# A graph layer with a mixture of experts on one core: the last chunk's slot tiles placed earlier, and the additions of results counted by gathers issued

## Chip, cores and metric

One core of one Trainium2 chip runs the whole kernel. The metric is device time in microseconds (us) of one execution. Six runs of the kernel before gave a median of 1196.74 us, from 1194.26 to 1201.27. One more execution was profiled: it took 1194.66 us, of which the profile covers a span of 1192.9 us.

The engines are named as in the profile: PE (TensorE), DVE (VectorE), ACT (ScalarE), POOL (GpSimd) and SP (SyncE). SP issues most of the plain transfers and POOL all the gathers.

## The reference

`x` has 6250 rows of 256 numbers, and there are 100000 edges `src -> dst`, sorted by `dst`.

```python
x = x + gnn(layernorm(x), edges, W, b)       # [h, mean of h[src] over the edges into a node] @ W.T + b
h = layernorm(x)
xn = layernorm(h) * gamma + beta
logits = xn @ Wr + br                        # 8 experts; the best two, softmax over those two
y = sum over the two: w_e * (gelu(xn @ W1[e] + b1[e]) @ W2[e] + b2[e])
x = x + y
```

Everything is float32. W1 is 256 x 512 for each expert, W2 is 512 x 256.

## The kernel before

**Windows, chunks, batches.** The edges are cut into 56 windows of 14 edge tiles (`C = 14`), 128 edges each. For an edge tile POOL gathers 128 rows of `z_d` (L601) into one of 28 buffers `xg` (`XG = 28`), issued 28 edge tiles ahead, and PE multiplies it with a one-hot matrix `hot` (L618). DVE makes the `hot` tiles of a window in two halves of seven (`hot_tiles`, L612). Four windows make a chunk (`CW = 4`); the 14 chunks lie in three batches of 8, 5 and 1 chunks (`BATCHES`).

**Routing a chunk.** When a window's sums stand in PSUM, DVE makes its new rows x1 (`window_x1`, L658 to L660). Behind a chunk's fourth window come: norms and logits, the choice of two experts, and the counts of tokens for each expert (`count_tokens`, L678 to L693). Then `one_hot_slots` (L697, L698) makes a tile `to` of 128 x 256 for each of the four windows on DVE, `sort_tokens` (L705, L708) multiplies the normed rows by it on PE and copies the result to `xs` on ACT. On DVE, `share_runs`, `place_rest` and `place_runs` (L727 to L780) work out where each expert's tokens go. ACT then copies the tokens to the experts' slots `xe` (`copy_runs`, L859). `find_rows` (L809 to L822) makes the plan: for each token the two rows of `y_d` with its results, and the two weights. `put_plan` (L826) writes it to DRAM in four transfers on SP; each of them overlaps the one before and so waits for its landing. `load_plans` (L841) reads it back.

**Experts.** A chunk's experts run in pairs (`expert_stages`: L884 and L889 for the hidden layer, L897 and L901 for the result, and a write of 256 rows to `y_d`, L903). Tokens beyond 128 for an expert go to rest tiles, which run behind a batch's last chunk (`more_stages`: L927 and L931, L936 and L939, L945 and L949, and a write to `y_d`, L952). The second batch has five rest tiles, the third two. The tiles `rows`, which L901, L931 and L949 write, rotate through three buffers; the PSUM tile `py` has one.

**Results.** The 49 node tiles of 128 rows are finished last. `gather_rows` loads x1 of a tile (L973, SP) and issues two gathers from `y_d` (L976, POOL): 98 in all. `add_rows` makes two additions with weights on DVE (L983) and writes the tile to the output (L985, SP). A tile's three buffers are taken in turn from the 28 of `xg`, so a buffer comes round again after nine node tiles. The gathers of a batch read `y_d` up to that batch's end, and so wait for its last write: 54 gathers are for the first batch, 36 for the second, 8 for the third.

**The order of work** is written by hand: every engine, SP's and POOL's queues among them, takes its instructions in the order in which this Python code issues them. One step of `after(t)` goes with each of the 784 edge tiles; when those are over, steps go on until nothing is left. `at(t, f)` puts a piece of work at a step; the tables `Steps`, `LateSteps` and `LastSteps` say at how many steps behind a chunk's last edge tile its pieces come. `after` also issues expert stages, paced by estimates of their times that it adds up in `clock`, and calls `sum_rows`. This issues the gathers of the next node tile when `clock` has reached `due`, and decides when the additions of earlier node tiles (the list `adds`) are issued.

In the kernel before, no addition is issued while edge tiles are left, unless more than eight node tiles wait (`XG // 3 - 1`). Behind them one is issued each time that `clock` has passed `added`, which goes up by 2.5 for each.

The last chunk, number 14, uses `LastSteps`: its four `to` tiles are issued at steps 13, 14, 17 and 18, its four sorts at 15, 16, 19 and 20, with `share_runs` at 15, `place_rest` at 16, `place_runs` at 19, the copies to slots from 21 on, `find_rows` at 22, and the first expert stages at 29.

Of the kernel before, what the change touches and what calls it, by code (L numbers as in the profile page):

```python
# [8 lines left out]
F32 = mybir.dt.float32  # L9
# [8 lines left out]
P = 128  # L18
EPS = 1e-5
C = 14  # L20
TB = 4
UB = 2
CW = 4
# [4 lines left out]
XG = 28  # L28
# [5 lines left out]
def gnn_ffn_kernel(ctx: ExitStack, tc: tile.TileContext, x, x_cols, src, dst, dst_next, gw, gw_t, gb, gb_cols, gamma, beta,  # L34
# [42 lines left out]
    W = src.shape[1]  # L77
# [511 lines left out]
    work = fast_pools.enter_context(tc.tile_pool(name="work", bufs=2, side="right"))  # L589
# [103 lines left out]
        nc.vector.tensor_scalar(q2, q2, -1.0, None, op0=ALU.add)  # L693

    def one_hot_slots(G, i):
        to = work.tile([P, 2 * P], F32, name="to", bufs=3)
        nc.vector.tensor_scalar(to, cols, G.to[:, 0, i:i + 1], None, op0=ALU.is_equal)  # L697
        nc.vector.scalar_tensor_tensor(to, cols, G.to[:, 1, i:i + 1], to, op0=ALU.is_equal, op1=ALU.add)  # L698
        G.one_hot[i] = to
# [269 lines left out]
    def gather_rows(K, n, V):  # L969
        V.rows = slice(n * P, min((n + 1) * P, N))  # L970
        count = V.rows.stop - V.rows.start
        V.o = spare()[:count]
        nc.sync.dma_start(V.o, x1_d[V.rows, :])  # L973
        V.y2 = [spare()[:count] for _ in range(2)]
        for r in range(2):
            nc.gpsimd.indirect_dma_start(  # L976
                out=V.y2[r], out_offset=None, in_=y_d[:K.batch.end_row, :],
                in_offset=bass.IndirectOffsetOnAxis(ap=plans[:count, n, r:r + 1], axis=0))

    def add_rows(n, V):  # L980
        count = V.rows.stop - V.rows.start
        for r in range(2):
            nc.vector.scalar_tensor_tensor(V.o, V.y2[r], plans.bitcast(F32)[:count, n, 2 + r:3 + r], V.o,  # L983
                                           op0=ALU.mult, op1=ALU.add)
        nc.sync.dma_start(out[V.rows, :], V.o)  # L985
# [3 lines left out]

    tasks, later, Ks, sums, adds = [], {}, [], [], []  # L990
    slots, w1_sb, w2_sb, xe = None, None, None, None
    now, spent, clock, due, added, spares = None, 0.0, 0.0, 0.0, 0.0, 0
    class Steps:

        x1, var, roots, norms, route, exps, weigh, choices, count = 2, 5, 7, 9, 11, 14, 15, 16, 19
        hot, sort = (22, 24, 26, 28), (26, 28, 30, 32)
        runs, rest, place, tiles, copied, rows, pace, start, apart = 30, 33, 36, 39, 40, 46, 1.5, 60, 2

    class LateSteps:

        x1, var, roots, norms, route, exps, weigh, choices, count = 2, 4, 5, 7, 9, 11, 12, 13, 15
        hot, sort = (17, 18, 20, 22), (19, 21, 23, 25)
        runs, rest, place, tiles, copied, rows, pace, start, apart = 20, 22, 24, 27, 26, 28, 1.25, 36, 1

    class LastSteps:

        x1, var, roots, norms, route, exps, weigh, choices, count = 2, 4, 5, 6, 7, 8, 9, 10, 12
        hot, sort = (13, 14, 17, 18), (15, 16, 19, 20)
        runs, rest, place, tiles, copied, rows, pace, start, apart = 15, 16, 19, 24, 21, 22, 1, 29, 1

    def at(t, f, *args):
        later.setdefault(max(t, now), []).append(lambda: f(*args))
# [1 line left out]
    def window_done(V, G, K, t):  # L1014
# [26 lines left out]
        for m in range(CW):  # L1041
            at(t + S.hot[m], one_hot_slots, G, m)
            at(t + S.sort[m], sort_tokens, G, m)
# [19 lines left out]

    def sum_rows():

        nonlocal due, added
        if now < W * C:
            added = clock + 3.0
        while adds and now >= W * C and (added <= clock or not (sums or tasks)):
            adds.pop(0)()  # L1070
            added += 2.5
        left = W * C - 1 - now
        while sums and not sums[0][0].batch.left and clock >= due and left < XG:
            if 0 < left < XG and spares + 3 > XG - left:
                return
            K, n = sums.pop(0)
            V = Group()
            gather_rows(K, n, V)
            adds.append(lambda n=n, V=V: add_rows(n, V))
            while len(adds) > XG // 3 - 1:  # L1080
                adds.pop(0)()
                added += 2.5
            due = max(due, clock - 6.0) + (4.0 if left > 0 else 2.4)

    def after(t):
        nonlocal now, spent, clock
        now = t
        while later.get(t):
            later[t].pop(0)()
        later.pop(t, None)  # L1090
        clock += 0.6 if t < W * C else 0.3 if tasks else 1.2

        pace = 0.6 if W * C - 56 <= t < W * C else 0.72 if t < W * C else 1.2 if len(Ks) < W // CW else 2.0
        spent = min(spent + pace, pace) if tasks else 0.0
        while tasks and spent > 0:
            us, f, _ = tasks.pop(0)
            spent -= us
            clock += us
            f()
        sum_rows()  # L1100
# [7 lines left out]
    now = 0  # L1108
# [62 lines left out]
    with tc.If(wrong_r > 0), tc.tile_pool(name="gp", bufs=1) as gp:  # L1171
# [9 lines left out]
        with tc.For_i(0, W * C) as j:  # L1181
# [22 lines left out]
            to = gp.tile([P, 1], I32, name="to")  # L1204
# [107 lines left out]
```

## Time and profile before

| what | us |
|---|---|
| six runs, median (lowest to highest) | 1196.74 (1194.26 to 1201.27) |
| the profiled execution: its own time | 1194.66 |
| its span in the profile | 1192.9 |
| busy: PE, PE's weight loads, DVE, ACT, POOL | 1055.5, 857.6, 687.9, 463.1, 843.8 |
| first and last start of the 98 gathers of results | 1049.9, 1180.5 |

The page lists for each engine its busy time, its share of 40 equal slices, the chain of work that ended last, and the costliest groups of instructions. The times of a timeline are us from the span's start. A line of it gives start, duration, engine, source line, operation, tiles and count; in brackets stand the idle time of the engine before it and what ended it. A row of windows gives for a stretch each engine's busy time, and behind them the share of full speed that the clock of PE was granted.

### The profile page before, as it was taken

What the parts mean: (1) busy time and instruction counts of PE and PEld (TensorE: products, weight loads), DVE (VectorE), ACT (ScalarE), POOL (GpSimd) and SP (SyncE); (2) the same over time, 40 slices, a digit from 0 to 9 for tenths busy, and PEclk for the clock granted to TensorE, in tenths of its full rate; (3) what the DMA queues carried; (4) which work ended last, traced back from release to release, by engine and by line L of the source; (5) the groups of instructions that cost most, each with busy time, mean ns of one, the idle gap of its engine ahead of it and who ended that gap; (6) DMA issues with size and microseconds to landing.
All of it is one profiled execution on the core that took longest, in us unless ns stands there. A gap on an engine that the chain in (4) does not pass through costs nothing.

```text
span 1192.9 us, 18881 instructions
## 1 busy us (share of the span) xinstructions
PE 1055.5 (88%) x5352; PEld 857.6 (72%) x5352; DVE 687.9 (58%) x2433; ACT 463.1 (39%) x1281; POOL 843.8 (71%) x892
## 2 busy tenths in 40 slices
PE   7939986899989989798998989899999999997970
PEld 6728765687868778686876868578888888785750
DVE  5747778564745645364564537465472745657652
ACT  3420002635434434344443444444553553643510
POOL 0077677777777777777777777777777777777674
PEclk9969988999999989899999999999999999998995
DMA  9978989546565555645555465555656564676874
GB/s 326 350 237 265 294 269 355 126 140 146 145 134 141 145 127 141 146 138 136 144 147 128 140 144 143 135 146 141 139 137 157 145 146 133 144 209 214 220 243 129
DMA packets 143578, 210.08 MB, mean 176 GB/s; under 512 B 36652, under 2 KB 111128, under 8 KB 143340
## 3 DMA queue, kind: packets, MB, share of 16 engines
q0 software_dynamic: 42768, 118.91, 40.4%
q1 hardware_dynamic: 92364, 80.45, 21.3%
q10 hardware_dynamic: 8336, 9.45, 2.4%
q8 instruction: 45, 0.74, 0.3%
q14 instruction: 65, 0.53, 0.1%
HBM read 163.86 MB, written 44.86 MB: 175 GB/s over the span
## 4 chain that ended last, share of the span: by engine, by line
PE 61%; DMA 14%; DVE 8%; ACT 4%; issue 3%; POOL 1%; ACTq 1%; SPq 0%; POOLq 0%; DVEq 0%
PE pS L618 21%; PE ph L884 16%; PE py L897 14%; DMA xg<-z_d,src_i 5%; PE pm L705 4%; DMA xg<-y_d,plans 3%; ACT xe L859 3%; DMA u_d<-u_t 3%; PE pS L621 2%; DMA plan_d<-plan 1%; PE ph L927 1%; PE py L945 1%; DMA x<-u_d 1%; DVE xe L863 1%; DVE xg L983 1%
## 5 line engine op out<-in xcount | busy, mean ns | idle before, releaser
L601 POOL DMA_INDIRECT xg<-z_d,src_i x770 | 731.7, 950 | 240.3 <-issue 103.6
L618 PE MATMUL pS<-xg,hot 128*128 128x265 f32 x1568 | 437.9, 404 | 53.9 <-DMA xg<-z_d,src_i 30.5
L618 PEld LDWEIGHTS pS<-xg,hot 128*128 128x128 f32 x1568 | 289.4, 195 | 135.1 <-DMA xg<-z_d,src_i 48.7
L884 PEld LDWEIGHTS ph<-xe,w_sb 128*128 128x128 f32 x1792 | 221.1, 196 | 13.1 <-ACT xe L859 4.5
L884 PE MATMUL ph<-xe,w_sb 128*128 128x128 f32 x1792 | 223.9, 280 | 2.9 <-ACT xe L859 2.9
L897 PE MATMUL py<-w_sb,hid 128*128 128x256 f32 x896 | 214.4, 383 | 1.8 <-DVE rows L901 1.8
L612 DVE TENSOR_TENSOR hot<-cols,rel 128x896 f32<-128x896 f32 x112 | 121.6, 1087 | 129.9 <-PE pS L618 127.3
L889 ACT ACTIVATE hid<-ph,b_sb 128x128 f32<-128x128 f32 x448 | 127.5, 368 | 173.3 <-PE ph L884 173.0
L897 PEld LDWEIGHTS py<-w_sb,hid 128*128 128x128 f32 x896 | 169.0, 191 | 33.3 <-issue 6.8
L859 ACT ACTIVATE xe<-xs x448 | 139.3, 311 | 86.3 <-ACT xe L859 36.6
L976 POOL DMA_INDIRECT xg<-y_d,plans x98 | 96.4, 984 | 36.1 <-issue 14.9
L708 ACT ACTIVATE xs<-pm,beta_sb,gamma_sb 128x256 f32<-128x256 f32 x112 | 57.1, 560 | 130.9 <-PE pm L705 130.5
L901 DVE TENSOR_TENSOR rows<-py,b_sb 128x512 f32<-128x512 f32 x56 | 38.4, 686 | 115.2 <-PE py L897 115.1
L640 ACT ACTIVATE sums<-pS 128x265 f32<-128x265 f32 x55 | 21.3, 388 | 114.2 <-PE pS L618 110.9
L271 PE MATMUL ph<-gc,x_t 128*128 128x264 f32 (+1 forms) x200 | 58.1, 416 | 8.1 <-ACT zt L295 5.0
L660 DVE SCALAR_TENSOR_TENSOR x<-pS,rdeg,x 128x264 f32<-128x264 f32 x55 | 27.1, 493 | 65.8 <-DMA x<-u_d 64.3
L705 PE MATMUL pm<-to,xn 128*128 128x256 f32 x224 | 58.6, 385 | 5.6 <-DVE to L698 5.6
L983 DVE SCALAR_TENSOR_TENSOR xg<-xg,plans,xg 128x256 f32<-128x256 f32 (+1 forms) x98 | 46.0, 485 | 21.9 <-DMA xg<-y_d,plans 18.1
L330 POOL DMA_INDIRECT xg<-x_dram,src_i x14 | 13.4, 958 | 61.0 <-DMA src_i<-src_dram 57.1
L271 PE MATMUL pm<-gc,x_t 128*128 128x264 f32 (+1 forms) x192 | 54.4, 408 | 0.0
L889 ACT ACT_TABLE_LOAD x25 | 32.1, 1283 | 56.3 <-PE ph L884 56.0
L271 PEld LDWEIGHTS ph<-gc,x_t 128*128 128x128 f32 x200 | 39.6, 202 | 18.8 <-ACT zt L295 5.9
(214 smaller groups left out, 892.1 us busy)
## 6 DMA issues: line engine op xcount, KB each, us to landing
y_d<-rows SPq DMA_DIRECT2D x56, 256.0 KB
xg<-z_d,src_i POOLq DMA_INDIRECT x770
w_sb<-w_dram ACTq DMA_DIRECT2D x16, 512.0 KB
x<-u_d SPq DMA_DIRECT2D x55, 132.0 KB
x_d<-x SPq DMA_DIRECT2D x55, 128.0 KB
u_d<-u_t SPq DMA_DIRECT2D x24, 264.0 KB
x_t<-x_cols_dram SPq DMA_DIRECT2D x12, 512.0 KB
xu<-x_dram SPq DMA_DIRECT2D x24, 256.0 KB
```

The costliest lines, as they stand in the source:

```text
L271: nc.tensor.matmul(pz, x_t[:, t, k, :], gc[:, h * KD + k, :n], start=(k == 0), stop=(k == KD - 1))
L601: nc.gpsimd.indirect_dma_start(out=xg[(g * C + c) % XG][:, :DZ], out_offset=None, in_=z_d[:, :], in_offset=bass.IndirectOffsetOnAxis(ap=sr ...
L612: nc.vector.tensor_tensor(hot, col[:, None, :].to_broadcast([P, HC, P]), V.rel[:, c:c + HC, None].to_broadcast([P, HC, P]), op=ALU.is_equal)
L618: nc.tensor.matmul(V.pS, V.hot[c // HC][:, c % HC, :], xg[(V.g * C + c) % XG], start=(c == 0), stop=(c == C - 1))
L705: nc.tensor.matmul(px[:, k, :], G.xn[i][:, k * P:(k + 1) * P], G.one_hot[i], start=True, stop=True)
L708: nc.scalar.activation(xs[:, at:at + 2 * P], px[:, k, :], AF.Identity, bias=beta_sb[:, k:k + 1], scale=gamma_sb[:, k:k + 1])
L859: nc.scalar.activation(xe[:, :, bass.ds(to_at, CAP)], src[:, :, bass.ds(src_at, CAP)], AF.Copy)
L884: nc.tensor.matmul(ph[:, i, a * SH:(a + 1) * SH], w1_sb[:, U.e + a, k, c * P:(c + 1) * P], xe[:, k, at:at + SH], start=(k == 0), stop=(k = ...
L889: nc.scalar.activation(U.hid[:, c, a * SH:(a + 1) * SH], ph[:, i, a * SH:(a + 1) * SH], AF.Gelu, bias=b1_sb[:, U.e + a, c:c + 1])
L897: nc.tensor.matmul(U.py[:, h, :], U.hid[:, c, h * P:(h + 1) * P], w2_sb[:, U.e + h, c, :], start=(c == 0), stop=(c == KH - 1))
L976: nc.gpsimd.indirect_dma_start(out=V.y2[r], out_offset=None, in_=y_d[:K.batch.end_row, :], in_offset=bass.IndirectOffsetOnAxis(ap=plans[:c ...
L983: nc.vector.scalar_tensor_tensor(V.o, V.y2[r], plans.bitcast(F32)[:count, n, 2 + r:3 + r], V.o, op0=ALU.mult, op1=ALU.add)
```

## The change

Three edits.

1. The tiles `to` get four buffers (`CW`) in place of three.
2. `LastSteps` places the last chunk's four `to` tiles at steps 13, 13, 14 and 15 and its sorts at 14 to 17; `share_runs`, `place_rest` and `place_runs` come at 16, 17 and 18, the copies from 20 on, `find_rows` at 21, the expert stages at 28.
3. `sum_rows` keeps no estimated time for additions. A node tile's additions are issued when more than three node tiles have had their gathers issued and wait for additions (more than five in the steps from the end of the edge tiles to the last chunk's last sort). This holds while edge tiles are left as well.

```diff
     def one_hot_slots(G, i):
-        to = work.tile([P, 2 * P], F32, name="to", bufs=3)
+        to = work.tile([P, 2 * P], F32, name="to", bufs=CW)
...
     class LastSteps:
         x1, var, roots, norms, route, exps, weigh, choices, count = 2, 4, 5, 6, 7, 8, 9, 10, 12
-        hot, sort = (13, 14, 17, 18), (15, 16, 19, 20)
-        runs, rest, place, tiles, copied, rows, pace, start, apart = 15, 16, 19, 24, 21, 22, 1, 29, 1
+        hot, sort = (13, 13, 14, 15), (14, 15, 16, 17)
+        runs, rest, place, tiles, copied, rows, pace, start, apart = 16, 17, 18, 24, 20, 21, 1, 28, 1
...
     def sum_rows():
-        nonlocal due, added
-        if now < W * C:
-            added = clock + 3.0
-        while adds and now >= W * C and (added <= clock or not (sums or tasks)):
+        nonlocal due
+        waiting = 5 if W * C <= now < W * C + LastSteps.sort[-1] else 3
+        while adds and (len(adds) > waiting or not (sums or tasks)):
             adds.pop(0)()
-            added += 2.5
         left = W * C - 1 - now
...
             adds.append(lambda n=n, V=V: add_rows(n, V))
-            while len(adds) > XG // 3 - 1:
-                adds.pop(0)()
-                added += 2.5
             due = max(due, clock - 6.0) + (4.0 if left > 0 else 2.4)
```

What this does to the order of the built program, engine by engine: up to the second batch's last stretch nothing moves. On DVE the two additions of node tile 0 come to stand ahead of the second half of the last window's `hot` tiles (they stood behind that window's expert results), and the additions of node tiles 1 to 5 ahead of that window's L658 (before: tiles 0 and 1). Tiles 6 to 10 stand between there and the counts (before: 2 to 7). The four `to` tiles come in a row, with two node tiles' additions among them; before, the third and fourth stood behind `place_rest` and an L931. On PE the four sorts (L705) come ahead of most of the second batch's L927. On SP the second write of a rest tile (L952) comes to stand behind the fourth `put_plan`; before, it stood behind the third. On POOL the 98 gathers keep their order.

More of the change, by code (lines that the diff above doesn't have):

```diff
@@ L991, in gnn_ffn_kernel @@
     slots, w1_sb, w2_sb, xe = None, None, None, None
-    now, spent, clock, due, added, spares = None, 0.0, 0.0, 0.0, 0.0, 0
+    now, spent, clock, due, spares = None, 0.0, 0.0, 0.0, 0
     class Steps:
```

## Prediction

> **What bounds the kernel now.** All that the change moves lies behind 1040 us, so I read the end first: the chain of work that ended last, in order of time.
>
> ```profile
> 1145.31 7.06 DMA xg<-y_d,plans x2
> 1153.07 16.19 DMA xg<-y_d,plans x5
> 1170.90 5.27 DMA xg<-y_d,plans
> 1180.50 5.97 DMA xg<-y_d,plans
> ```
>
> Its rows are start and time spent. The end hangs on gathers of results. POOL's timeline shows why:
>
> ```profile
> 1049.89 0.94 POOL L976 DMA_INDIRECT xg<-y_d,plans  x1 [0.30 <-PE pS L618]
> 1051.14 0.94 POOL L976 DMA_INDIRECT xg<-y_d,plans  x1 [0.30 <-DMA xg<-z_d,src_i]
> ...
> 1117.88 0.94 POOL L976 DMA_INDIRECT xg<-y_d,plans  x1 [3.87 <-DMA out_dram<-xg]
> ...
> 1124.95 0.94 POOL L976 DMA_INDIRECT xg<-y_d,plans  x1 [1.52 <-DVE xg L983]
> ```
>
> 98 gathers stand in one queue, one each 1.25 us (0.94 and 0.30), from 1049.89 on. 97 steps would take 121.3 us; the last started at 1180.50, after 130.6. Some 6.2 us of the rest are four stops above the usual 0.30 (0.69 at 1109.14, 3.57, 0.73 and 1.22), the others are single slow starts. The gather at 1124.95 is number 55, the first for the second batch: it needs that batch's last write to `y_d`. SP's timeline (start, time that the entries last, number of transfers) shows when that went out:
>
> ```profile
> 1105.01 0.35 SPq L826 DMA_DIRECT2D plan_d<-plan  x1
> ...
> 1109.13 3.39 SPq L826 DMA_DIRECT2D plan_d<-plan  x2
> 1112.61 0.38 SPq L952 DMA_DIRECT2D y_d<-rows  x1
> ...
> 1116.04 0.34 SPq L826 DMA_DIRECT2D plan_d<-plan  x1
> ...
> 1119.77 0.93 SPq L952 DMA_DIRECT2D y_d<-rows  x2
> ```
>
> The last write was issued at 1120.3. With some 3.5 us to land (1120.3 to 1123.8) it explains 1124.95, though the profile names DVE. So the stops at 1109 to 1121 are hidden: without them POOL would stand at gather 55 until the same moment. **The second batch's last write to y_d, then POOL's queue, sets the end.** The first of the last chunk's gathers, number 91, started at 1170.90; that chunk's last L952 was issued at 1159.5. There are some 9 us of slack.
>
> **Part 1: additions by gathers issued (edit 3).** DVE takes its queue in order, so an addition issued early holds all behind it until its gather has landed.
>
> ```profile
> 1046.17 1.09 DVE L612 TENSOR_TENSOR hot<-cols,rel 128x896 f32<-128x896 f32 x1 [6.31 <-PE pS L618]
> ...
> 1061.73 0.15 DVE L658 TENSOR_SCALAR rdeg<-pS 128x1 f32<-128x1 f32 x1
> ```
>
> *First wait.* Node tile 0's two additions now stand ahead of this `hot` tile. Its second gather starts at 1051.14; a gather on the chain took 3.64 us (`1088.07 3.64 DMA xg<-y_d,plans` among its rows): 1054.8. One addition (0.48) and the tile (1.09): ready at 1056.4, not 1047.3. PE needs it for the last window's eighth edge tile, at 1052.7 (three edge tiles in 1.51 us from 1052.22). **PE stands for 3.7 us**, with the expert matmuls queued behind. After such an idle stretch PE runs slowly for a while; the windows of 1074 to 1082 show it behind an idle time of 3.64 us (a row has the busy time of PE, its weight loads, DVE, ACT and POOL, then PE's granted clock, the DMA engines' busy share and GB/s):
>
> ```profile
> 1074.00:1078.00 4.00, 1.89 (x8) 1.66 (x9) 3.76 (x15) 1.46 (x5) 3.08 (x4) 0.86 0.96 325
> 1078.00:1082.00 4.00, 3.12 (x10) 2.06 (x10) 2.35 (x7) 0.00 (x0) 3.09 (x4) 0.72 0.50 149
> ```
>
> The granted clock falls to 0.86 and 0.72, and eight L897 matmuls took 3.52 us there against 1.89 later: +1.6 to +2.2. So the last window's sums come 5.3 to 5.9 later.
>
> *Second wait.* Tiles 1 to 5 are added ahead of L658. Tile 5's second gather is number 12: 1049.89 + 11 x 1.25 = 1063.6, landed 1067.3, added 1067.8, against 1061.73: +6.1. Both ways give **+6.0 for L658**. From there to the counts (L680, 1076.89) the work stays, 15.2 us, with five node tiles' additions in place of six (0.92 less), which waits for ACT eat up: counts at 1082.9, **+6.0** (from +5.1 to +6.5).
>
> On SP each write to the output now comes earlier, with the next tile's load of x1 (L973) behind it. That load is needed three node tiles later, 7.5 us by POOL's pace, and takes some 3: no cost while landings stay under that; if they don't, an addition waits for the rest.
>
> **Part 2: slot tiles early (edits 1 and 2).** This gains. Before:
>
> ```profile
> 1092.62 0.48 DVE L697 TENSOR_SCALAR to<-cols,q 128x256 f32<-128x256 f32 x1
> ```
>
> PE had waited 3.90 us for the third tile and then ran slowly, and the copies to slots came behind the fourth sort, at 1100.61. Now DVE goes through without that. From L901 (1080.14 before) to the end of `place_runs` (1097.6) it took 17.5 us; now, from 1086.2, the pieces add up to: two L901 and L931 1.8, four `to` 3.7, four node tiles 3.7, `share_runs` 1.5, a table load 0.6, `place_rest` 2.9, `place_runs` 1.5, together 15.7. `place_runs` ends at 1101.9 (+4.3) and the copies start at 1102.3: **+1.7 only; 4 of the 6 us are won back.** The fourth buffer costs nothing (an earlier chunk's order is the same).
>
> **Part 3: the plan's transfers on SP.** Behind 1101.9 come two L931 (1.2), four node tiles (3.7) and `find_rows` (1.9): the plan stands at 1108.7, +3.7 against 1104.98. Its first transfer goes at about 1110.6, behind the first rest tile's write. The others wait for each other's landing: 3.68 us apart in the rows above, 3.13, 3.64 and 3.00 in rows of the chain at 557 to 564; I take 3.4. The fourth goes at 1120.8. The second rest tile's write to `y_d`, ready at 1113.5, now stands behind it in SP's queue (before: behind the third, at 1112.61): 1121.4, landed some 2.9 us later, 1124.3. The fourth rest tile's L949 needs the buffer of `rows` that this write reads: **1124.4, not 1116.46.** PE's fifth rest result needs the one `py` buffer: it starts 0.5 later, after 4.5 us idle, slowly (four matmul pairs, 3.4 us), so the fifth L949 comes at 1128.5 against 1119.04: **+9.4**.
>
> The Trainium skill, DMA: Bandwidth & Descriptors, section on the anatomy of one DMA, gives about 2.0 us of fixed cost for a transfer. Three waits of that length would put the fourth transfer 4.2 us earlier, and an estimate by the page would bring the whole change to about +5 us. The rows of 3.0 to 3.68 us stand against it.
>
> **Part 4: POOL.** From the fifth L949's end to gather 55 it took 5.5 us before, 0.8 of it in SP's queue. Now 1128.9 and 4.0 (write at once, land, restart): 1132.9, against 1124.95: **+8.0**. Gather 91 would follow at 1132.9 + 36 x 1.25 = 1177.9. By then the last chunk has to be done. PE starts it at 1128.3 (+9.5), and its L901 on DVE now stand behind additions that wait for POOL: the first behind tile 28 (gather 58: 1136.7, landed 1140.3) at 1140.7, against 1129.64; the second behind tile 33 (gather 68, 1149.2) at 1153.1, against 1136.66. PE waits there again, some 4 us and slowly. From the second L901 to the last landing it took 25 us before (1136.66 to about 1161.7); with the slow stretch that gives 1179, and gather 91 at about 1179.3. **+1.4.** The slack of 9 us is used up.
>
> **Sum.** 8.0 + 1.4 = +9.4 on the profiled execution's 1194.66: 1204.1. That execution lies 2.1 below the median of the runs shown, so a median of **1206**. Ends of the unknowns: transfers of the plan 2.4 us apart and landings of 2.6 give about +3.5; landings near the 5.27 of the chain's slow row give +13. So 1200 to 1210 for this case.
>
> **Rivals.**
> - *Faster: POOL's queue runs through.* The sorts' gain reaches the second batch's end whole: PE loses neither the 3.90 us before the third sort nor some 1.9 in slow clock, its last write goes out 5.8 earlier, and the hidden stops (6.2) become real gain: 1194.66 - 6.2 + 2.1 = 1190.5. It decides if part 1 costs less than the sorts win, thus if the first additions are released before PE needs the `hot` tile (1052.7). Against it: the gather alone starts at 1051.14. 0.12.
> - *No change.* Part 1 comes as worked out, but the second rest tile's write gets past SP in time (transfers of the plan faster, or a buffer free earlier): then only the +1.7 to +3.7 of parts 2 and 3 reach gather 55, and the last chunk keeps slack. 1196.7 + 0 to 3.6: 1197 to 1200. 0.16.
> - *Slower still.* The last chunk's L901 wait longer than in part 4, and gather 91 with them: +14 and more, 1211 and up. 0.04.
>
> The forecast has 0.68. About 0.3% (3.6 us) is what a measurement of this kernel can tell from no change. Slower: forecast and the last rival, and a little of the second: 0.74; within 0.3%: 0.14; faster 0.12. The range must leave out no more than 0.2: from 1197, with the case of no change, to 1211.
>
> **What would show it.** In the new profile: the last window's second `hot` tile at about 1055 with additions ahead of it; PE idle there and a granted clock under 0.8; L658 at about 1068; the `to` tiles in one row at 1087 to 1092; the second rest tile's L952 behind the fourth L826, at about 1121; one stop of some 15 us in POOL's queue ahead of gather 55, at about 1133, and none before it. I am wrong if that gather starts before 1126, or if PE runs through at 1053.

## The result, and the profile after

The changed kernel took 1205.49 us (median of 20 runs, 1202.41 to 1209.76), the kernel before 1197.34 us beside it (46 runs): **ratio 1.007, 95% interval 1.0059 to 1.008**, some 8 us slower. The profiled execution's span is 1204.5 us against 1192.9.

The end of the chain of waits (start, time spent) again hangs on gathers of results, now in a nearly unbroken row:

```profile
1136.67 11.30 DMA xg<-y_d,plans x4
1152.02 9.10 DMA xg<-y_d,plans x3
1164.52 5.09 DMA xg<-y_d,plans
...
1192.31 5.71 DMA xg<-y_d,plans
```

POOL's timeline has only two long stops. The four stops of before up to gather 55 have become one of 14.61 us ahead of gather 55, the first for the second batch. A second one, ahead of gather 91, the first for the last chunk, is new:

```profile
1050.39 0.95 POOL L976 DMA_INDIRECT xg<-y_d,plans  x1 [0.30 <-PE pS L618]
...
1134.04 1.07 POOL L976 DMA_INDIRECT xg<-y_d,plans  x1 [14.61 <-DVE xg L983]
...
1182.86 0.94 POOL L976 DMA_INDIRECT xg<-y_d,plans  x1 [3.41 <-DMA xg<-x_d]
```

The releasers named here are not the ones that count: gather 55 needs the second batch's last write, issued at 1131.58, and gather 91 the last chunk's, issued at 1179.1. SP's timeline shows the four transfers of the plan 3.1 to 3.7 us apart, and the second rest tile's write (1123.62) right behind the fourth:

```profile
1113.15 0.35 SPq L826 DMA_DIRECT2D plan_d<-plan  x1
...
1116.86 0.34 SPq L826 DMA_DIRECT2D plan_d<-plan  x1
...
1120.08 0.34 SPq L826 DMA_DIRECT2D plan_d<-plan  x1
...
1123.19 0.34 SPq L826 DMA_DIRECT2D plan_d<-plan  x1
1123.62 0.38 SPq L952 DMA_DIRECT2D y_d<-rows  x1
...
1131.58 0.32 SPq L952 DMA_DIRECT2D y_d<-rows  x1
```

On DVE node tile 0's additions hold the second `hot` tile: DVE stands 13.17 us until the first of their gathers has landed. L658 comes at 1069.35, behind the last of the additions of tiles 1 to 5:

```profile
1056.07 0.48 DVE L983 SCALAR_TENSOR_TENSOR xg<-xg,plans,xg 128x256 f32<-128x256 f32 x1 [13.17 <-DMA xg<-y_d,plans]
1056.78 0.48 DVE L983 SCALAR_TENSOR_TENSOR xg<-xg,plans,xg 128x256 f32<-128x256 f32 x1 [0.23 <-DMA xg<-y_d,plans]
1057.18 1.08 DVE L612 TENSOR_TENSOR hot<-cols,rel 128x896 f32<-128x896 f32 x1
...
1068.95 0.48 DVE L983 SCALAR_TENSOR_TENSOR xg<-xg,plans,xg 128x256 f32<-128x256 f32 x1 [0.70 <-DMA xg<-y_d,plans]
1069.35 0.15 DVE L658 TENSOR_SCALAR rdeg<-pS 128x1 f32<-128x1 f32 x1
```

PE stands 2.47 us for the `hot` tile, which ends at 1058.26 (the row of PE names L658 of the window before, which runs beside it). PE's granted clock (in the second row, behind POOL's busy time) is 0.57 in the next window:

```profile
1058.32 2.13 PE L618 MATMUL pS<-xg,hot 128*128 128x265 f32 x4 [2.47 <-DVE rdeg L658]
```

```profile
1058.00:1062.00 4.00, 3.68 (x9) 2.96 (x10) 3.76 (x11) 0.00 (x0) 3.09 (x4) 0.57 0.71 208
```

In the last chunk the first expert result (L901) still waits for PE (0.48 us). From the second on they stand on DVE behind additions that wait for gathers:

```profile
1152.91 0.48 DVE L983 SCALAR_TENSOR_TENSOR xg<-xg,plans,xg 128x256 f32<-128x256 f32 x1 [1.22 <-DMA xg<-y_d,plans]
1154.45 0.52 DVE L983 SCALAR_TENSOR_TENSOR xg<-xg,plans,xg 128x256 f32<-128x256 f32 x1 [1.05 <-DMA xg<-y_d,plans]
1154.90 0.68 DVE L901 TENSOR_TENSOR rows<-py,b_sb 128x512 f32<-128x512 f32 x1
```

Part of the shift in this trace is older than the change: the first batch's first L952 goes out at 781.62, against 778.60 before. So 3.0 us come off PE's, DVE's and SP's times when this trace is compared with before; POOL's queue doesn't share the shift (gather 1 at 1050.39 and 1049.89). A second trace of the changed kernel, below, starts level.

Eight of the runs below were measured in two sessions in which the kernel before took 1414 to 1416 us; why is not known (the record has one chip number, 12, both for one of these sessions and for the later ones at 1196 us). A gather (L601) lasts as long there as elsewhere (951 ns, 950 in the profile of before), but the engines stand more between instructions (POOL idle 419.2 us ahead of these gathers in place of 240.3). From the page of edits 1 and 2 alone, measured in such a session:

```profile
L601 POOL DMA_INDIRECT xg<-z_d,src_i x770 | 732.4, 951 | 419.2 <-issue 171.4
```

Those runs are `sorts_alone`, `adds_alone`, `first_gone`, `second_gone`, `both_gone`, `late_gone`, `spread` and `sorts_spread`. Their ratios hold against the kernel before in the same session; their times aren't set against the others.

### The profile page after: what moved, and what is told of

It reads as the page before. It is cut to its first block, busy times and chain, and to the rows that moved or that the text cites. A ratio compares the mean times of both kernels' runs of the same rounds, so it can differ in the third digit from the quotient of the medians.

```text
span 1204.5 us, 18875 instructions
## 1 busy us (share of the span) xinstructions
PE 1064.5 (88%) x5352; PEld 865.6 (72%) x5352; DVE 687.7 (57%) x2433; ACT 463.2 (38%) x1281; POOL 844.4 (70%) x892
## 4 chain that ended last, share of the span: by engine, by line
PE 62%; DMA 14%; DVE 6%; ACT 4%; issue 3%; POOL 1%; ACTq 1%; SPq 0%; POOLq 0%; DVEq 0%
PE pS L618 23%; PE ph L884 15%; PE py L897 13%; DMA xg<-z_d,src_i 5%; DMA xg<-y_d,plans 4%; PE pm L705 4%; ACT xe L859 3%; DMA u_d<-u_t 3%; PE pS L621 2%; PE py L945 2%; PE ph L927 1%; DMA x<-u_d 1%; DMA plan_d<-plan 1%; PE ph L271 1%; DVE xg L983 1%
## 5 line engine op out<-in xcount | busy, mean ns | idle before, releaser
L601 POOL DMA_INDIRECT xg<-z_d,src_i x770 | 732.3, 951 | 240.7 <-issue 112.4
L618 PE MATMUL pS<-xg,hot 128*128 128x265 f32 x1568 | 438.8, 406 | 52.1 <-DMA xg<-z_d,src_i 27.2
L618 PEld LDWEIGHTS pS<-xg,hot 128*128 128x128 f32 x1568 | 291.1, 197 | 131.9 <-DMA xg<-z_d,src_i 43.2
L884 PEld LDWEIGHTS ph<-xe,w_sb 128*128 128x128 f32 x1792 | 225.9, 200 | 14.5 <-ACT xe L859 5.7
L884 PE MATMUL ph<-xe,w_sb 128*128 128x128 f32 x1792 | 228.4, 283 | 4.0 <-ACT xe L859 4.0
L897 PE MATMUL py<-w_sb,hid 128*128 128x256 f32 x896 | 217.1, 387 | 6.6 <-DVE rows L901 6.6
L897 PEld LDWEIGHTS py<-w_sb,hid 128*128 128x128 f32 x896 | 171.0, 193 | 39.3 <-issue 9.5
L901 DVE TENSOR_TENSOR rows<-py,b_sb 128x512 f32<-128x512 f32 x56 | 38.4, 686 | 99.4 <-PE py L897 99.1
L705 PE MATMUL pm<-to,xn 128*128 128x256 f32 x224 | 57.5, 380 | 1.7 <-DVE to L698 1.7
```

Source lines behind the costliest of these rows:

```text
L601: nc.gpsimd.indirect_dma_start(out=xg[(g * C + c) % XG][:, :DZ], out_offset=None, in_=z_d[:, :], in_offset=bass.IndirectOffsetOnAxis(ap=sr ...
L618: nc.tensor.matmul(V.pS, V.hot[c // HC][:, c % HC, :], xg[(V.g * C + c) % XG], start=(c == 0), stop=(c == C - 1))
L705: nc.tensor.matmul(px[:, k, :], G.xn[i][:, k * P:(k + 1) * P], G.one_hot[i], start=True, stop=True)
L884: nc.tensor.matmul(ph[:, i, a * SH:(a + 1) * SH], w1_sb[:, U.e + a, k, c * P:(c + 1) * P], xe[:, k, at:at + SH], start=(k == 0), stop=(k = ...
L897: nc.tensor.matmul(U.py[:, h, :], U.hid[:, c, h * P:(h + 1) * P], w2_sb[:, U.e + h, c, :], start=(c == 0), stop=(c == KH - 1))
```

## Experiments

**Theory W**: edit 3 makes the loss, by additions that hold DVE. **Rival S**: the new steps make it, through SP's order. **Rival T**: the slot tiles (edits 1 and 2) gain 5 to 6 us once edit 3 is taken away. **P and Q**: one of the two waits in the last window makes the loss by itself (P: PE's stop and slow clock; Q: the additions ahead of L658).

### The changed kernel a second time

> The changed kernel itself, unchanged, beside the kernel before on the same chip, so that the other runs can be held against it on a chip where everything takes longer (1415 us for the kernel before, its engines standing between instructions). If the loss is a fixed number of microseconds made by the additions' places, it is +8 to +15 us there too (ratio 1.006 to 1.011); on a chip with the kernel before at 1197 us it is +8.2 again (1.006 to 1.008). Rival (the loss hangs on the delays of this one state, the waits of the last window above all): on the slower chip less than +4 us, a ratio under 1.003.

Measured beside a kernel before at 1195.62: 1203.74 us, **1.0064 (1.0042 to 1.0087)**. The span is 1200.4, its first L952 at 778.49, level with before. Gathers 55 and 91:

```profile
1129.36 1.06 POOL L976 DMA_INDIRECT xg<-y_d,plans  x1 [12.62 <-DVE xg L983]
...
1178.62 0.94 POOL L976 DMA_INDIRECT xg<-y_d,plans  x1 [3.83 <-DVE xg L983]
```

They are 4.4 and 7.7 us later than before (1124.95, 1170.90): over half of the loss is there at gather 55, the rest is added by the last chunk.

### Edits 1 and 2 alone

```diff
-        hot, sort = (13, 14, 17, 18), (15, 16, 19, 20)
-        runs, rest, place, tiles, copied, rows, pace, start, apart = 15, 16, 19, 24, 21, 22, 1, 29, 1
+        hot, sort = (13, 13, 14, 15), (14, 15, 16, 17)
+        runs, rest, place, tiles, copied, rows, pace, start, apart = 16, 17, 18, 24, 20, 21, 1, 28, 1
...
-        to = work.tile([P, 2 * P], F32, name="to", bufs=3)
+        to = work.tile([P, 2 * P], F32, name="to", bufs=CW)
```

First in a session of the 1415 us kind, then in one with the kernel before at 1196:

> The kernel before with edits 1 and 2 alone (slot tiles early, four buffers), its additions by the clock. Theory W (the loss is made by additions that hold DVE, edit 3): with it gone the last window's sums (L658) are back near 1061.7 and the counts near 1076.9, no later than before. Gather 55 does not move much: its writes stand behind the plan's transfers and the additions as before. 1195 to 1199 us. Rival S (the loss is made by the new steps of the last part, through SP's order of plan and result transfers): 1200 to 1205 us, with the second rest tile's L952 behind the fourth L826. Rival T (the slot tiles' gain, 5.8 us, reaches the end when nothing takes it back): 1190 to 1192 us, gather 55 before 1121.

> Edits 1 and 2 alone again, on a chip with the kernel before at 1196 us. Theory W (edit 3 makes the loss): L658 at 1061 to 1063 and the counts at 1076 to 1078, no stop of PE at the last window's eighth edge tile; the second batch's last write still stands behind the plan's transfers and the results' stops, so gather 55 stays within 2 us of 1125: 1194 to 1199 us. Rival T (the slot tiles' gain reaches the end once nothing takes it back): 1188 to 1192 us. Rival S (the new steps make the loss): 1200 to 1205 us.

Measured: 1.0025 (0.9995 to 1.0054) and **1.0009 (0.9993 to 1.0025)**, no difference either time; 1197.48 against 1195.60 us in the second. So edit 3 makes the loss, S falls, and T falls as well. What became of the slot tiles' gain stands in the second trace. L658 is at 1061.60, as before (1061.73), and the plan is ready early, at 1100.94 against 1104.82. Then SP takes the gain away. This is its queue (the second L826 row ends at 1113.39, when its second transfer has been let through), and DVE's fourth and fifth L949:

```profile
1109.18 4.21 SPq L826 DMA_DIRECT2D plan_d<-plan  x2
1113.49 0.38 SPq L952 DMA_DIRECT2D y_d<-rows  x1
```

```profile
1117.11 0.42 DVE L949 TENSOR_TENSOR rows<-py,b_sb 128x256 f32<-128x256 f32 x1 [5.47 <-DMA y_d<-rows]
1121.07 0.42 DVE L949 TENSOR_TENSOR rows<-py,b_sb 128x256 f32<-128x256 f32 x1 [3.53 <-PE py L945]
```

The second rest tile's write stands behind the fourth transfer of the plan, the fourth L949 waits 5.47 us for it, and PE for that. The fifth L949 comes at 1121.07, later than before (1119.04), gather 55 at 1124.73 (1124.95).

### Edit 3 alone

The changed kernel with the two lines of `LastSteps` and `bufs=3` as they were.

> The kernel before with edit 3 alone, its old steps for the last part. Theory W: the whole loss of the change is here, and what the early slot tiles win back inside it (some 4 us by the prediction's part 2) is missing: 1206 to 1211 us, L658 at 1067 to 1070, gather 55 at 1133 or later. Rival S: the loss needs the new steps; without them 1196 to 1200 us. Under rival T as well 1209 to 1212 us.

Measured in a 1415 us session: **1.0108 (1.0069 to 1.0146)**, slower, as W says; S falls a second time.

### The last window's waits, one at a time and both

Three kernels, each with one of the three lines, in this order: `first_gone`, `second_gone`, `both_gone` (and again as `both_gone_2`).

```diff
-        waiting = 5 if W * C <= now < W * C + LastSteps.sort[-1] else 3
+        waiting = 8 if now < (W - 1) * C else 5 if W * C <= now < W * C + LastSteps.sort[-1] else 3
+        waiting = 8 if (W - 1) * C <= now < W * C + LastSteps.sort[-1] else 3
+        waiting = 8 if now < W * C + LastSteps.sort[-1] else 3
...
             adds.append(lambda n=n, V=V: add_rows(n, V))
+            while len(adds) > XG // 3 - 1:
+                adds.pop(0)()
```

> The changed kernel, but node tile 0's two additions stand behind the last window's second hot tile, as the only thing moved. The prediction says that two waits end nearly together: then taking the first away alone leaves the second. PE runs through at 1053 to 1058 at full clock, but L658 still waits for the additions of tiles 1 to 5, whose last gather is number 12: L658 stays at 1066 to 1069. Theory W: 1203 to 1206 us, at most 2.5 us less than the changed kernel (the expert matmuls behind PE's stop come earlier). Rival P (PE's idle time and slow clock make the loss, the additions none): 7 us come back, 1197 to 1200 us.

> The changed kernel, but the additions of tiles 1 to 5 come later: up to eight tiles may wait, from the last window on until its part's fourth sort. Tile 0's additions still stand ahead of the second hot tile. Theory W with two parallel waits: PE's stop is still there and brings L658 at 1065 to 1068; the postponed additions fall due in a row behind the sorts. 1203 to 1208 us, no less than 2.5 us under the changed kernel. Rival P gives the same, 1204 to 1206. Rival Q (the second wait alone makes the loss): 1198 to 1201 us and L658 at 1062 to 1063.

> The changed kernel with both waits of the last window gone: up to eight tiles wait from the start until the last part's fourth sort, then three as in the change. Theory W: L658 is back at 1061 to 1063 and the counts at 1076 to 1078. What is left of the change's loss is what the additions do from the slot tiles on: five tiles' additions fall due in a row there, the last chunk's L901 still stand behind additions that wait for POOL. 1199 to 1203 us, between the two kernels. Rival (the loss is made in the last window only): 1196 to 1198 us, or less by the sorts' gain.

Measured in 1415 us sessions: 1.0079 (1.0048 to 1.011), 1.0071 (1.0048 to 1.0094), 1.0092 (1.006 to 1.0123). These can't decide between P, Q and two parallel waits. The first gather stands 14 to 17 us ahead of the last window's second `hot` tile there, where it was 6.8 us in the first trace of the changed kernel; in the trace of edit 3 alone that tile waits for PE (6.08 us), not the other way. P and Q stay open as to size. But these runs show that the loss needs no stop of PE in the last window. Which of the two waits ends last where both are there, the two traces of the changed kernel show: L658 comes right behind tile 5's second addition, 1.8 and 1.7 us after PE's last L618 of that window.

> The changed kernel with both waits of the last window gone, again, on a chip with the kernel before at 1196 us. If parts 1 and 2 of the prediction are right, L658 is at 1061 to 1063 and the counts at 1076 to 1078, and what is left are the additions from the slot tiles on: those put off fall due there in a row, the second rest tile's L952 still stands behind the fourth L826, and the last chunk's L901 behind additions that wait for POOL. 1199 to 1203 us: half of the loss from the last window, half from behind it. Rival (the last window makes it all): 1194 to 1198 us. Rival (the last window makes none of it): 1203 to 1206 us.

Measured beside a kernel before at 1195.60: 1202.47 us, **1.0051 (1.0035 to 1.0067)**. This trace starts 4.0 us late (first L952 at 782.60). L658 at 1065.74 is then exactly where it was before, and PE runs through at full clock:

```profile
1058.00:1062.00 4.00, 4.00 (x18) 2.85 (x17) 0.42 (x2) 0.00 (x0) 3.08 (x4) 1.00 0.57 174
```

Yet most of the loss remains. (The traced execution is the slowest of the twelve, 1206.53 us.) DVE's timeline between `place_runs` and the plan shows one part of it: five node tiles are added in one row of ten additions, and two more stand behind the next L931. None of them waits; it is DVE's own time.

```profile
1103.83 4.65 DVE L983 SCALAR_TENSOR_TENSOR xg<-xg,plans,xg 128x256 f32<-128x256 f32 x10
1108.40 0.68 DVE L931 COPY rows<-ph 128x512 f32<-128x512 f32 x1
1109.00 1.92 DVE L983 SCALAR_TENSOR_TENSOR xg<-xg,plans,xg 128x256 f32<-128x256 f32 x4
```

The plan (L822) comes 3.7 us later than before (1112.56, less 4.0, against 1104.82), nearly the same as in the two traces of the changed kernel (3.4 and 3.7). Counted in DVE's timelines, 15 node tiles' additions stand ahead of it before, 14 with edits 1 and 2 alone, and 19 in all three traces with edit 3. Against edits 1 and 2 alone (1100.94; this trace starts 4.1 us later than that one) the plan is 7.5 us later. Of these, 4.6 us lie between `place_runs` and the plan, where seven node tiles stand in place of two. The other 2.9 us lie between L658 and `place_runs`, where both kernels add the same number of tiles; there PE was slow for longer. This is the second L897 behind the counts, from the chain of work that ended last:

```profile
1085.60 3.75 PE py L897 x8
```

It took 1.97 us in the traces of before, of edits 1 and 2 alone and of the changed kernel; here the granted clock is 0.50 from 1082 to 1090. The trace of `sorts_spread_2` below, without edit 3, has the same, so these 2.9 us are not shown to be edit 3's. The last chunk goes as in the changed kernel (gather 91 at 1182.87). By the ratios the two waits are worth the distance of 1.0051 from 1.007 and 1.0064, some 2 us; the intervals overlap, so even that is not shown. How the rest divides between the row of additions and the last chunk isn't shown either.

### Additions late behind the sorts

```diff
+        waiting = 3 if now < W * C else 5 if now < W * C + LastSteps.sort[-1] else 8
```

> The changed kernel with its additions up to the fourth sort, and up to eight tiles waiting from then on. Both waits of the last window stay: L658 at 1067 to 1070. The last chunk's L901 no longer stand behind additions that wait for POOL, and the plan and the rest tiles no longer behind additions. Theory W with the prediction's parts 3 and 4: gather 55 comes at 1128 to 1131, gather 91 some 45 us after it without a stop: 1199 to 1203 us. Rival (the last window's delay reaches the end whole): 1204 to 1206 us.

Measured in a 1415 us session: 1.0061 (1.0034 to 1.0089). It is the lowest ratio with edit 3 in these sessions but its interval overlaps all the others: inconclusive.

### The plan's transfers apart

```diff
-        runs, rest, place, tiles, copied, rows, pace, start, apart = 16, 17, 18, 24, 20, 21, 1, 28, 1
+        runs, rest, place, tiles, copied, rows, pace, start, apart = 16, 17, 18, 24, 20, 21, 1, 28, 3
...
-        sums.extend((K, n) for n in K.nodes)
+        if K.first + CW < W:
+            sums.extend((K, n) for n in K.nodes)
...
         at(t + S.start, start_experts, K)
+        if K.first + CW == W:
+            at(t + S.rows + 2 + CW * S.apart, lambda: sums.extend((K, n) for n in K.nodes))
```

This was put into the changed kernel (`spread`), and into the kernel with edits 1 and 2 alone (`sorts_spread`, `sorts_spread_2`).

> The changed kernel with the four transfers of the last plan three steps apart in place of one, and the last chunk's sums joined to the queue behind them; nothing else moves. The rest tiles' L952 no longer stand behind the fourth L826. The prediction's part 3 puts a large part of the loss on SP's order: the fourth L949 comes at 1118 to 1121 in place of 1126.8, PE doesn't stand for it, gather 55 at 1128 to 1130: 1199 to 1202 us. Rival (SP's order is no bound, DVE's additions hold the rest tiles anyway): 1204 to 1206 us.

> The kernel before with the slot tiles early (edits 1 and 2) and the plan's transfers three steps apart, no edit 3. If SP's order is what keeps the slot tiles' gain from gather 55, it comes here: the second batch's last write some 4 us earlier, gather 55 at 1120 to 1122, POOL's queue then without a long stop: 1191 to 1194 us. If POOL's own queue or DVE bounds instead: 1195 to 1198 us.

> The kernel before with edits 1 and 2 and the plan's transfers three steps apart, no edit 3, on a chip with the kernel before at 1196 us. If SP's order of plan and result transfers keeps the slot tiles' gain from gather 55, it comes here: the rest tiles' L952 no longer behind L826, gather 55 at 1120 to 1122, gather 91 some 45 us later: 1191 to 1194 us. If DVE or POOL's own queue bounds instead: 1195 to 1198 us, as without the spread.

Measured in a 1415 us session: 1.0086 (1.006 to 1.0112) for `spread`, no nearer to before than the other kernels with edit 3, and 1.0036 (1.0006 to 1.0066) for `sorts_spread`. For the second, with the kernel before at 1195.60: 1194.64 us, **0.9976 (0.9959 to 0.9993)**, the only version below both kernels. SP's queue there:

```profile
1112.07 0.34 SPq L826 DMA_DIRECT2D plan_d<-plan  x1
1112.51 0.38 SPq L952 DMA_DIRECT2D y_d<-rows  x1
...
1116.02 0.35 SPq L826 DMA_DIRECT2D plan_d<-plan  x1
```

The write goes out behind the second transfer. This trace starts 1.5 us late; less that, gather 55 is at 1123.7, 1.2 us earlier than before and 1.1 than without the spread. The expectation's 1120 to 1122 is missed, and its 1191 to 1194 us narrowly. Here `place_runs` ended 3.0 us later than with edits 1 and 2 alone: the second L897 behind the counts took 3.75 us in place of 1.97, at a granted clock of 0.50. In the 1415 us session there is no such gain: 1.0036 is slower than before.

## Why the prediction was right, and where it was not

The time (1206 forecast, 1205.49 measured) and most of the steps came out. The first trace of the changed kernel is given less its 3.0 us of earlier shift, but for the gathers and what hangs on them (from gather 55 on) the raw time stands in brackets.

| step | forecast | first trace | second trace |
|---|---|---|---|
| second `hot` tile ready | 1056.4 | 1055.3 | 1055.8 |
| PE stands for it | 3.7 | 2.5 | 3.1 |
| L658 | 1067.8 | 1066.4 | 1066.6 |
| counts (L680) | 1082.9 | 1082.4 | 1082.6 |
| `place_runs` ends | 1101.9 | 1101.7 | 1102.0 |
| plan (end of L822) | 1108.7 | 1108.4 | 1108.7 |
| second rest tile's L952 | 1121.4 | 1120.6 | 1119.5 |
| fifth L949 | 1128.5 | 1128.1 | 1126.4 |
| gather 55 | 1132.9 | 1131.0 (1134.0) | 1129.4 |
| last chunk's second L901 | 1153.1 | 1151.9 (1154.9) | 1150.1 |
| gather 91 | 1179.3 | 1179.9 (1182.9) | 1178.6 |
| end of span (1192.9 + 9.4) | 1202.3 | 1201.5 (1204.5) | 1200.4 |

- **Part 1, two waits: there, but the loss doesn't need them.** Both waits are in the trace at their places, and the second ends last. In the changed kernel they make most of the plan's delay: against edits 1 and 2 alone L658 is 4.6 and 5.0 us later (first and second trace), the plan 7.2 and 7.6. But with both gone the loss is still 1.0051. What edit 3 still fixes there is how many node tiles are added ahead of the plan: 19 in place of 15. If DVE doesn't wait for them early, it does them in a row later, at 0.93 us a tile (4.65 for five). That this row carries the loss is read from one trace; no run isolates it. PE's stop was shorter than forecast (2.5 and 3.1 us for 3.7). Its slow stretch had the size forecast, 1.6 to 2.2: four L618 took 2.13 us in place of 1.16 and eight L897 2.59 and 2.52 in place of 1.89, together +1.7 and +1.6.
- **Part 2 was right.** In the first trace's own times the four `to` tiles stand between 1088.95 and 1094.5, and from the L901 ahead of them (1088.35) to the end of `place_runs` it takes 16.3 us, 15.7 forecast and 17.5 before. The sum's "table load" of 0.6 is no row of the profile: before, DVE stood 0.57 us there, which the profile calls "issue"; now it stands 0.88 us for an L927.
- **Part 3 was right in mechanism.** The second rest tile's write stands behind the fourth transfer in both traces; with edits 1 and 2 alone this order leaves nothing of the gain at gather 55, and the spread, which undoes it, brings 2.8 us (1197.48 to 1194.64), about half of the 5 to 6 us expected. The distance of 3.4 us between transfers is 3.71, 3.22 and 3.11 in the first trace; in the second it is 3.36, 3.58 and then 1.58, which brings the fifth L949 2.1 us earlier than forecast. The section of the Trainium skill that the prediction cites for 2.0 us (DMA: Bandwidth & Descriptors, Anatomy of one DMA) is on transfers issued by GpSimd. These are SP's, and all of their distances but one lie above 2.0.
- **Part 4: two sizes off, against each other.** Gather 55 starts 2.5 us behind the last write's issue in both traces (1131.58 to 1134.04, 1126.88 to 1129.36), not 4.0: +8.0 was too much, it is +6.1 and +4.4. In the kernel before this distance is 4.65 us (1120.3 to 1124.95), and ahead of gather 91 it is 3.8 and 4.7 (1179.1 to 1182.86, 1173.9 to 1178.62): it is no fixed time, and whether the last write alone ended the stop at gather 55 before is not shown. From gather 55 to gather 91 it takes 48.8 and 49.3 us against 46.0 before, +2.9 and +3.3 for a forecast of +1.4. The additions ahead of the last chunk's L901 are for 29, 34, 37 and 39 node tiles, before for 26, 29, 32 and 35.
- **The faster rival had the wrong condition.** It was to decide if part 1 costs less than the sorts win. In `sorts_alone_2` part 1 costs nothing, and the ratio is 1.0009: SP's order has to go too, and even then 0.24% is what comes. That the time came out is in part luck: in part 4 one size was too large and the other too small.
- **The rival of no change** let the write past SP in time. In the changed kernel that order was mended only in a 1415 us session, where it brought nothing to be seen. What it brings at 1196 us with edit 3 in place wasn't run, nor was the price of the last chunk's additions alone.

## What to carry to other kernels

On an engine that takes its queue in order, a limit on unfinished work is a promise to do that work ahead of everything issued later; count how much of it stands ahead of the instructions that release others (here the plan and L901), before looking for single waits. A wait that is taken away gives little back if the same work then falls due in a row ahead of the same instruction (here 1.0051 in place of 1.0064 to 1.007). And a stage made earlier on one engine gains only as far as the next queue lets its results out: here a plan 3.9 us earlier on DVE came to nothing (1.0009) with four chained 2 KB transfers on SP ahead of the result's write.

## What the runs showed of the hardware

- In the last chunk the chained transfers of the plan were mostly 2.9 to 4.5 us apart (without the spread, in the traces at 1196 to 1206 us), but once 1.58 (1117.51 to 1119.09).
- PE fell to about half clock behind 2.47 us of standing (0.57) in the first trace and to 0.70 and 0.87 in neighbouring windows behind 3.09 us in the second. The Trainium skill, TensorE: Matmul & The Clock Gate, Part 1 on the HAM clock gate, gives at least one idle window, about 3.4 us, for the fall to half clock. The half agrees; the traces show the fall behind a shorter stop too.
- The slow stretch is not equally long each time: behind a stop of PE of 3.60 to 3.87 us ahead of the counts (L678), the second group of eight L897 took 1.97 us in four traces and 3.75 in two (`both_gone_2`, `sorts_spread_2`), whose stops were 3.60 and 3.72.
- Two executions of the same work reach the same instruction up to 4 us apart (the first L952 at 778.46 to 782.60) before the code differs: differences of that size in a single trace need a common point ahead of the change.
